# Relative attention: near-diagonal terms for 64 positions at a time over four row groups, and a new table of steps

## The chip, the core and the metric

The kernel runs on one NeuronCore of a Trainium2 chip. Its engines run side by side: TensorE (PE; its weight loads are listed as PEld), VectorE (DVE), ScalarE (ACT), GpSimd (POOL), and SyncE (SP), which starts the DMAs here. Each works through its own instructions in order and waits for others by semaphores. The metric is the device time of one execution in microseconds; 4292.06 us is the median of three runs (4282.06, 4292.06, 4292.41).

## What is computed

Four sublayers on x (16 sequences, 256 positions, 128 features, fp32), each followed by a residual sum and a layer norm: attention with relative positions, a stack of six local-attention layers, a causal attention, and experts. The change touches the first:

```
rel = clip(r[:, None] - r[None, :], -64, 64) + 64
q, k, v = heads(x @ Wq), heads(x @ Wk), heads(x @ Wv)          # 16 heads of 8
content = einsum('bhld,bhmd->bhlm', q, k)
rel_k   = einsum('bhld,lmd->bhlm', q, Ek[rel])
rel_q   = einsum('bhmd,lmd->bhlm', k, Eq[rel])
logits  = (content + rel_k + rel_q + pos_pos) * scale           # pos_pos from Eq, Ek alone
attn    = softmax(logits)
out     = attn @ v + einsum('bhlm,lmd->bhld', attn, Ev[rel])
x       = layernorm(x + out)
```

The terms rel_q and rel_k depend on l - m through a small table that is constant beyond a distance of 64. They are made apart for the two diagonal 128 x 128 blocks of the logits ("near the diagonal") and for corners of the other blocks.

## The kernel before: how the work is staged

`relative_attention` (line 243) works on 16 batches. A batch has eight units: unit u has the 128 rows l of half lc = u // 4 and four heads. Each unit runs three steps: `weights` (L493) builds the logits of four heads in one PSUM tile `big` by transposing the rel_k terms into it (L505) and adding q times k over two 32-row groups of PE (L517), after which DVE adds the rel_q terms and finds the least (L527); `exponentials` (L539) on ACT; `turn_weights` (L552) transposes the result on PE (L562) into two `small` tiles, which ACT or DVE copies out (L566, L568).

PSUM has eight banks: two `big` tiles of two banks each and four `small` tiles of one bank, each kind handed out in turn. A step that takes the next tile of a kind waits until the readers of its last content are done.

Once a batch come the other steps. `turn` and `project` make x transposed, q and k. `diagonal` (L375) multiplies x by spread weights (64 matmuls, L388) and DVE masks the result into the tile `r_d` (L396): in each group of 32 partitions the head features of four neighbouring positions stand block by block, so that one matmul over 32 rows gives the terms of four positions, for all heads and both halves. `diagonal` "k" serves the rel_q terms (`rq_...`), `diagonal` "q" the rel_k terms (`rk_...`); both use the one tile `r_d`. `chunk` (L403) makes the near-diagonal terms of 32 positions: eight matmuls of 32 rows and 128 columns (L413), four quads g times two x, with x in two row groups and two banks of one `big`. `rows_of` (L372) says which row group holds which 16 positions. `rq_chunk` (L445) copies them out by two ACT copies of 128 x 512 (L449), `rk_chunk` (L465) by two DVE additions (L470). Four chunks cover 128 positions, so a batch has four of each. `corners` (L422) makes the other terms, 16 matmuls over all four row groups (L434) a call, two calls of each kind. `positions` (L570), `values` (L606), `join`, `statistics` and `normalise` are the output side; `spread_k` is work of POOL, `project_v` makes v.

The order is written by hand: `TURNS` (L669) has eight turns, one for each unit, and each turn lists its steps with how many units (for the three steps of a unit) or batches they lie behind; -1 means one batch ahead. `run` (L742) goes through the turns, and `in_order` (L204) keeps each of PE, ACT, DVE and POOL in that order. The first four turns run before the last tables are set up (L815), the rest after.

Of the kernel before, what the change touches and what calls it, by code (L numbers as in the profile page):

```python
# [19 lines left out]
P = 128  # L20
NB, S, D = 16, 256, 128
NT = S // P
H, HD = 16, 8
# [81 lines left out]
def bcast(ap, shape):  # L105
    return ap.to_broadcast(list(shape))
# [3 lines left out]
def transformer_kernel(ctx: ExitStack, tc: tile.TileContext, I, out: bass.AP):  # L110
# [93 lines left out]
    def in_order(first):  # L204
# [25 lines left out]
        third=third,  # L230
    )
    relative_attention(tc, I, xb, env)
    wp = ctx.enter_context(tc.tile_pool(name="wp", bufs=2))
    wq = ctx.enter_context(tc.tile_pool(name="wq", bufs=1))
# [8 lines left out]
def relative_attention(tc, I, xb, env):  # L243
# [13 lines left out]
    V, A, G, T = nc.vector, nc.scalar, nc.gpsimd, nc.tensor  # L257
    big, small, ident = env.big, env.small, env.ident
# [3 lines left out]
    C0 = P - 4  # L262
    E0 = MAXD - 4

    with ExitStack() as ctx:
# [5 lines left out]
        rq3, rk3, rkc3 = [None] * 3, [None] * 3, [None] * 3  # L271
# [10 lines left out]
        tq = one.tile([P, NTAB], F32, name="r_tq")  # L282
        tk = one.tile([P, NTAB], F32, name="r_tk")
# [4 lines left out]
        pp = one.tile([P, P], F32, name="r_pp")  # L288
# [19 lines left out]
        def of(three, b, lc):  # L308
            return three[lc * (1 + b % 2)]

        st = {b: {} for b in range(NB)}
# [60 lines left out]
        def rows_of(s_, r):  # L372
            return r if s_ else r ^ 2
# [26 lines left out]
            )  # L400
            st[b]["d", n] = d

        def chunk(table, d, c):  # L403

            ps = big()
            for g in range(4):
                for x in range(2):
                    at = 8 * c + 4 * x + g
                    s_ = at // 16
                    r = rows_of(s_, at // 4 % 4)  # L410
                    o = C0 - 4 * at
                    rows = slice(32 * r, 32 * r + 32)
                    T.matmul(  # L413
                        ps[:, 512 * x + 128 * g : 512 * x + 128 * g + 128],
                        lhsT=table[rows, o : o + P],
                        rhs=d[rows].rearrange("p h t s g i -> p (h t) s g i")[:, :, s_, g, :],
                        start=True,
                        stop=True,
                    )
            return ps  # L420

        def corners(tables, d, halves, upper, phase):  # L422

# [18 lines left out]
                "p x (g h i) -> p x g h i", g=4, i=4  # L442
            )

        def rq_chunk(b, c):  # L445
            ps = chunk(tq, st[b]["d", "k"], c).rearrange("p (g h t i) -> p t g h i", g=8, t=NT, i=4)
            for t in range(NT):
                o = of(rq3, b, t)[:, :, 0, 32 * c : 32 * c + 32]
                A.copy(o.rearrange("p h (g i) -> p g h i", i=4), ps[:, t])  # L449

        def rq_corners(b, phase):

# [9 lines left out]
                    ps[rows],  # L462
                )

        def rk_chunk(b, c):  # L465
            ps = chunk(tk, st[b]["d", "q"], c).rearrange("p (g h t i) -> p t g h i", g=8, t=NT, i=4)
            pc = pp[:, 32 * c : 32 * c + 32].rearrange("p (g i) -> p g i", i=4).unsqueeze(2)
            for t in range(NT):
                o = of(rk3, b, t)[:, :, 32 * c : 32 * c + 32]
                V.tensor_add(  # L470
                    o.rearrange("p h (g i) -> p g h i", i=4), ps[:, t], bcast(pc, (P, 8, H, 4))
                )

        def rk_corners(b, phase):
# [184 lines left out]
        def normalise(b, lc):  # L659
# [8 lines left out]
        UNIT = (weights, exponentials, turn_weights)  # L668
        TURNS = (  # L669
            (  # L670
                (1, values, 0),
                (0, rk_corners, 1),
                (-1, turn),
                (0, rk_chunk, 1),
                (2, turn_weights),
                (0, rk_chunk, 0),
                (0, rk_corners, 0),
                (-1, project),
                (1, exponentials),
                (-1, diagonal, "k"),  # L680
                (0, weights),
            ),
            (
                (2, turn_weights),
                (0, weights),
                (1, exponentials),
            ),
            (
                (0, weights),
                (1, positions, 1),  # L690
                (2, turn_weights),
                (1, join, 0),
                (1, exponentials),
            ),
            (
                (1, exponentials),
                (0, weights),
                (-1, rq_chunk, 1),
                (1, values, 1),
                (2, turn_weights),  # L700
                (-1, rq_corners, 1),
                (-1, rq_chunk, 2),
            ),
            (
                (1, exponentials),
                (1, join, 1),
                (0, weights),
                (-1, rq_chunk, 0),
                (2, turn_weights),
                (-1, spread_k, 0),  # L710
            ),
            (
                (2, turn_weights),
                (1, exponentials),
                (1, statistics, 1),
                (0, weights),
            ),
            (
                (-1, rq_chunk, 3),
                (0, positions, 0),  # L720
                (1, normalise, 1),
                (-1, rq_corners, 0),
                (1, exponentials),
                (-1, diagonal, "q"),
                (0, weights),
                (-1, rk_chunk, 3),
                (2, turn_weights),
                (0, project_v),
                (1, statistics, 0),
            ),  # L730
            (
                (1, exponentials),
                (2, turn_weights),
                (0, weights),
                (1, normalise, 0),
                (-1, spread_k, 1),
                (-1, rk_chunk, 2),
            ),
        )
        N = NB * NU  # L740
# [13 lines left out]
        with tc.tile_pool(name="r_setup", bufs=1) as su, tc.tile_pool(  # L754
# [32 lines left out]
            def toeplitz(dst, ext):  # L787

                ps = small()
                for j in range(4):  # L790
                    o = S - 1 - C0 - j
                    T.matmul(
                        ps[:, 0:NTAB],
                        lhsT=sel[:, j, :],
                        rhs=ext[:, o : o + NTAB],
                        start=(j == 0),
                        stop=(j == 3),
                    )
                V.tensor_scalar_mul(dst, ps[:, 0:NTAB], -scale)
                return ps  # L800

            ps = toeplitz(tq, extq)
# [22 lines left out]
            ps = small()  # L825
# [38 lines left out]
            for dst, n, src, d, width, parts, end in (  # L864
# [6 lines left out]
                for i in range(0, width, 512):  # L871
                    n_ = min(512, width - i)
                    ps = small()
# [1083 lines left out]
```

## Time and profile before

| | |
|---|---|
| median of three runs | 4292.06 us |
| profiled execution, its own time | 4290.48 us |
| span of its profile, first to last instruction | 4288.7 us |
| relative attention on PE | from 17 to 820 us |
| PE, DVE, ACT, POOL busy in 85 to 820 us | 719.65, 442.50, 448.80, 143.53 us of 735 |
| matmul records of `chunk` (L413) in 85 to 775 us | some 1,870, 0.27 us each by the record |
| granted PE clock 25 to 38, 38 to 47, 47 to 62 us | 0.61, 0.64, 0.53 |
| granted PE clock 85 to 820 us | 1.00 |

An fp32 matmul leaves two records. Records overlap, since PE is pipelined: what a step costs PE is the time from its first start to the next step's first start, and this is what the prediction uses. A line of the timeline merges neighbouring records of one line of code: start, length, engine, line, operation, output and inputs, contraction rows * columns of the weights, shape of the moving operand, count. "issue" is idle time in which the engine waited for nothing that the profile shows.

### The profile page before, as it was taken

How to read it: one execution, taken by the hardware profiler on the slowest of the kernel's cores; microseconds unless marked ns; L12 is line 12 of the kernel's file. 1: busy time of each engine (PE TensorE's matmuls, PEld its weight loads, DVE VectorE, ACT ScalarE, POOL GpSimd, SP SyncE). 2: the span in 40 equal slices, each digit the busy share in tenths (PEclk: the TensorE clock that was granted, in tenths of full speed). 3: DMA queues.
4: the chain of work that ended last, by engine and by line, in shares of the span. 5: the costliest groups of instructions: out<-in, count | busy, mean ns of one | idle time of the engine just before them, and what ended most of it. 6: DMA issues, size and time to landing. Idle time of an engine off the chain costs nothing.

```text
span 4288.7 us, 149072 instructions
## 1 busy us (share of the span) xinstructions
PE 4167.7 (97%) x62028; PEld 3051.9 (71%) x62028; DVE 3321.3 (77%) x6347; ACT 3293.4 (77%) x11368; POOL 2698.4 (63%) x3176
## 2 busy tenths in 40 slices
PE   8999999889999999999999999999999999989997
PEld 6888888667677777667776677776766777656665
DVE  4655665588888888888888888888888888769974
ACT  3666566488888888888888888888888888769973
POOL 2121211388888888888888888888888888623321
PEclk8999999999999999999999999999999999989998
DMA  1000000100000000000000000000000000000000
GB/s 35 3 3 3 3 3 3 49 25 15 20 20 23 19 20 19 25 19 15 20 19 24 20 21 19 24 18 16 19 15 24 15 15 14 9 2 2 2 8 20
DMA packets 158799, 69.51 MB, mean 16 GB/s; under 512 B 123549, under 2 KB 154276, under 8 KB 158124
## 3 DMA queue, kind: packets, MB, share of 16 engines
q1 hardware_dynamic: 158124, 59.99, 5.6%
q8 instruction: 488, 8.00, 0.8%
q14 instruction: 187, 1.53, 0.1%
HBM read 21.72 MB, written 2.12 MB: 6 GB/s over the span
## 4 chain that ended last, share of the span: by engine, by line
PE 91%; POOL 3%; issue 2%; ACT 2%; DVE 2%; DMA 0%; SPq 0%; POOLq 0%; ACTq 0%; DVEq 0%
PE small L1240 15%; PE big L1090 15%; PE small L1147 7%; PE big L1215 7%; PE big L1162 6%; PE small L1215 3%; PE small L1337 3%; PE small L1321 3%; PE big L505 3%; PE small L562 3%; PE small L1578 3%; PE small L1305 3%; PE big L1534 3%; PE big L517 3%; PE big L413 2%
## 5 line engine op out<-in xcount | busy, mean ns | idle before, releaser
L1183 ACT ACTIVATE a_pr<-a_pr,a_nb 128x64 f32<-128x64 f32 x3072 | 1023.8, 338 | 6.6 <-DVE a_nb L1176 6.6
L1111 POOL TENSOR_TENSOR a_u<-a_u,a_r 128x1024 f32<-128x1024 f32 x384 | 900.7, 2367 | 51.9 <-DVE a_r L1106 51.9
L1129 POOL TENSOR_TENSOR a_u<-a_u,a_y 128x1024 f32<-128x1024 f32 x384 | 722.4, 1902 | 15.0
L1240 PE MATMUL small<-a_vo,a_g 128*128 128x128 f32 x6144 | 719.2, 275 | 2.6 <-ACT a_g L1233 2.6
L1240 PEld LDWEIGHTS small<-a_vo,a_g 128*128 128x128 f32 x6144 | 702.6, 192 | 4.5 <-ACT a_g L1233 4.4
L1101 ACT ACTIVATE a_sq<-big 128x1024 f32<-128x1024 f32 x384 | 391.1, 1020 | 304.8 <-PE big L1090 304.5
L1183 ACT ACTIVATION_READ_ACCUMULATOR a_pr<-a_pr,a_nb 128x1 f32 x3072 | 587.9, 191 | 0.0
L1118 DVE TENSOR_REDUCE a_ss<-a_sq 128x16 f32<-128x1024 f32 x384 | 446.6, 1202 | 0.0
L1147 PE MATMUL small<-ident,a_u 128*128 128x128 f32 x3072 | 402.3, 274 | 12.9 <-POOL a_u L1129 12.9
L1090 PE MATMUL big<-w_k,a_xs 128*128 128x512 f32 x768 | 385.4, 624 | 2.2 <-DMA w_k<-in_L_ffn_Wqkv_dram 1.7
L1147 PEld LDWEIGHTS small<-ident,a_u 128*128 128x128 f32 x3072 | 346.4, 141 | 50.6 <-POOL a_u L1129 32.4
L1195 POOL TENSOR_TENSOR a_pr<-a_pr,a_rd 128x1024 f32<-128x1024 f32 x192 | 365.5, 1904 | 16.7 <-DVE a_rd L1194 16.5
L1090 PE MATMUL big<-w_q,a_xs 128*128 128x512 f32 x768 | 360.9, 592 | 0.0
L1162 PEld LDWEIGHTS big<-a_kT,a_qT 64*32 64x32 f32 x24576 | 262.5, 105 | 130.0 <-issue 71.1
L1170 DVE TENSOR_TENSOR a_pr<-big,w_band 128x1024 f32<-128x1024 f32 x192 | 234.7, 1222 | 110.4 <-PE big L1162 110.4
L527 DVE CUSTOM_DVE_ANT_0 r_lg<-big,r_rq 128x256 f32<-128x256 f32 x512 | 186.9, 421 | 155.5 <-PE big L517 67.4
L1162 PE MATMUL big<-a_kT,a_qT 64*32 64x64 f32 x24576 | 295.5, 226 | 10.5 <-POOL a_kT L1140 5.5
L1102 DVE TENSOR_TENSOR a_u<-big,a_tak 128x1024 f32<-128x1024 f32 x192 | 235.0, 1224 | 86.3 <-ACT a_sq L1101 82.8
L1223 ACT COPY a_g<-big 128x1024 f32<-128x1024 f32 x192 | 194.4, 1012 | 115.8 <-PE small L1215 115.2
L1215 PE MATMUL small<-a_pT,a_xm 32*128 32x512 f32 x768 | 282.4, 643 | 0.2 <-DVE xa L1247 0.2
L1090 PEld LDWEIGHTS big<-w_q,a_xs 128*128 128x128 f32 x768 | 145.5, 190 | 185.2 <-issue 129.5
L1215 PE MATMUL small<-a_pT,a_xt 32*128 32x512 f32 x768 | 262.8, 592 | 0.0
(276 smaller groups left out, 9482.0 us busy)
## 6 DMA issues: line engine op xcount, KB each, us to landing
a_xm<-a_xt SPq DMA_DIRECT2D x96, 96.0 KB
f_xt<-xa SPq DMA_DIRECT2D x96, 64.0 KB
f_xt<-xa SPq DMA_DIRECT2D x96, 63.5 KB
a_xt<-xa SPq DMA_DIRECT2D x80, 64.0 KB
a_xt<-xa SPq DMA_DIRECT2D x80, 63.5 KB
w_k<-in_L_ffn_Wqkv_dram SPq DMA_DIRECT2D x6, 512.0 KB
w_q<-in_L_ffn_Wqkv_dram SPq DMA_DIRECT2D x6, 512.0 KB
w_v<-in_L_ffn_Wqkv_dram SPq DMA_DIRECT2D x6, 512.0 KB
```

What stands on the lines that cost most here:

```text
L1090: T.matmul(ps[:, c * 512 : (c + 1) * 512], lhsT=xs_of[i, b][:, t, 0:P], rhs=weights[i]["qk"[j]][:, c * 512 : (c + 1) * 512], start=True, s ...
L1101: A.activation(sq, ps3, AF.Square)
L1102: V.tensor_mul(u, ps3, bcast(ta[:, t].unsqueeze(1), (P, H, DH)))
L1111: G.tensor_add(u, u, r)
L1118: V.tensor_reduce(ss[:, j], st[m]["sq", j], AX.X, ALU.add)
L1129: G.tensor_mul(u, u, bcast(y[:, j].unsqueeze(2), (P, H, DH)))
L1147: T.transpose(ps[:, k, :], u[:, o : o + P], ident)
L1162: T.matmul(ps[q0 : q0 + WIN, e, c, :], lhsT=qT[DH * e : DH * (e + 1), c, q0 : q0 + WIN], rhs=kT[DH * e : DH * (e + 1), c, t * P + q0 : t * ...
L1183: A.activation(s_["pr"][:, h], s_["pr"][:, h], AF.Exp, bias=s_["nb"][:, h : h + 1], accum_out=s_["den"][:, h : h + 1],)
L1195: G.tensor_mul(s_["pr"], s_["pr"], bcast(rd.unsqueeze(2), (P, H, DH)))
L1215: T.matmul(ps[win], lhsT=x[r, t, :], rhs=pT[r, :, o, :], start=(o == 0), stop=(o == 1),)
L1240: T.matmul(ps[:, 0:D], lhsT=st[m]["g"][:, h, :], rhs=weights[i]["vo"][:, h // 2, h % 2, :], start=(h == 0), stop=(h == H - 1),)
```

## The change

`chunk` becomes `diagonals`, which makes the terms of 64 positions in one go: 16 matmuls of the same shape, in the order quad g, then c over the four row groups. Group c writes its own bank: two of one `big`, and two `small` tiles. The evictions go tile by tile: for the `big` two instructions of 128 x 512 elements, for each `small` two of 128 x 256, six a half in place of four for two chunks. `rq_chunk` and `rk_chunk` become `rq_half` and `rk_half`, two of each for a batch. `TURNS` is written anew: the halves stand in turns 4 and 5 (rq), 7 and 0 (rk), and other steps move too: `values` and `diagonal` "k" in turn 0, `join`, `rq_corners`, `rk_corners`, `spread_k`, `diagonal` "q", `positions`, `statistics`, `normalise` and `project_v` as the diff shows. The sum of the matmuls and of the elements evicted stays.

```diff
--- before.py
+++ after.py
@@ -400,24 +400,29 @@
             )
             st[b]["d", n] = d
 
-        def chunk(table, d, c):
-
-            ps = big()
+        def diagonals(table, d, s_):
+
+
+
+            both = big()
+            ps = [both[:, 0:512], both[:, 512:1024], small(), small()]
             for g in range(4):
-                for x in range(2):
-                    at = 8 * c + 4 * x + g
-                    s_ = at // 16
-                    r = rows_of(s_, at // 4 % 4)
-                    o = C0 - 4 * at
+                for c in range(4):
+                    r = rows_of(s_, c)
+                    o = C0 - 4 * (16 * s_ + 4 * c + g)
                     rows = slice(32 * r, 32 * r + 32)
                     T.matmul(
-                        ps[:, 512 * x + 128 * g : 512 * x + 128 * g + 128],
+                        ps[c][:, 128 * g : 128 * g + 128],
                         lhsT=table[rows, o : o + P],
                         rhs=d[rows].rearrange("p h t s g i -> p (h t) s g i")[:, :, s_, g, :],
                         start=True,
                         stop=True,
                     )
-            return ps
+            for n, p_ in ((8, both), (4, ps[2]), (4, ps[3])):
+                at = 64 * s_ + (0 if n == 8 else 32 if p_ is ps[2] else 48)
+                p_ = p_.rearrange("p (g h t i) -> p t g h i", g=n, t=NT, i=4)
+                for t in range(NT):
+                    yield t, at, n, p_[:, t]
 
         def corners(tables, d, halves, upper, phase):
 
@@ -442,11 +447,10 @@
                 "p x (g h i) -> p x g h i", g=4, i=4
             )
 
-        def rq_chunk(b, c):
-            ps = chunk(tq, st[b]["d", "k"], c).rearrange("p (g h t i) -> p t g h i", g=8, t=NT, i=4)
-            for t in range(NT):
-                o = of(rq3, b, t)[:, :, 0, 32 * c : 32 * c + 32]
-                A.copy(o.rearrange("p h (g i) -> p g h i", i=4), ps[:, t])
+        def rq_half(b, s_):
+            for t, m0, n, p_ in diagonals(tq, st[b]["d", "k"], s_):
+                o = of(rq3, b, t)[:, :, 0, m0 : m0 + 4 * n]
+                A.copy(o.rearrange("p h (g i) -> p g h i", i=4), p_)
 
         def rq_corners(b, phase):
 
@@ -462,13 +466,12 @@
                     ps[rows],
                 )
 
-        def rk_chunk(b, c):
-            ps = chunk(tk, st[b]["d", "q"], c).rearrange("p (g h t i) -> p t g h i", g=8, t=NT, i=4)
-            pc = pp[:, 32 * c : 32 * c + 32].rearrange("p (g i) -> p g i", i=4).unsqueeze(2)
-            for t in range(NT):
-                o = of(rk3, b, t)[:, :, 32 * c : 32 * c + 32]
+        def rk_half(b, s_):
+            for t, l0, n, p_ in diagonals(tk, st[b]["d", "q"], s_):
+                pc = pp[:, l0 : l0 + 4 * n].rearrange("p (g i) -> p g i", i=4).unsqueeze(2)
+                o = of(rk3, b, t)[:, :, l0 : l0 + 4 * n]
                 V.tensor_add(
-                    o.rearrange("p h (g i) -> p g h i", i=4), ps[:, t], bcast(pc, (P, 8, H, 4))
+                    o.rearrange("p h (g i) -> p g h i", i=4), p_, bcast(pc, (P, n, H, 4))
                 )
 
         def rk_corners(b, phase):
@@ -668,73 +671,69 @@
         UNIT = (weights, exponentials, turn_weights)
         TURNS = (
             (
-                (1, values, 0),
                 (0, rk_corners, 1),
                 (-1, turn),
-                (0, rk_chunk, 1),
                 (2, turn_weights),
-                (0, rk_chunk, 0),
-                (0, rk_corners, 0),
+                (0, rk_half, 0),
                 (-1, project),
+                (-1, diagonal, "k"),
+                (1, values, 0),
                 (1, exponentials),
-                (-1, diagonal, "k"),
                 (0, weights),
             ),
             (
+                (0, weights),
                 (2, turn_weights),
-                (0, weights),
-                (1, exponentials),
-            ),
-            (
-                (0, weights),
-                (1, positions, 1),
-                (2, turn_weights),
-                (1, join, 0),
                 (1, exponentials),
             ),
             (
                 (1, exponentials),
                 (0, weights),
-                (-1, rq_chunk, 1),
-                (1, values, 1),
+                (1, positions, 1),
                 (2, turn_weights),
-                (-1, rq_corners, 1),
-                (-1, rq_chunk, 2),
             ),
             (
                 (1, exponentials),
-                (1, join, 1),
+                (1, join, 0),
                 (0, weights),
-                (-1, rq_chunk, 0),
+                (-1, rq_corners, 1),
+                (1, values, 1),
                 (2, turn_weights),
-                (-1, spread_k, 0),
             ),
             (
-                (2, turn_weights),
+                (1, join, 1),
+                (-1, rq_corners, 0),
                 (1, exponentials),
                 (1, statistics, 1),
                 (0, weights),
+                (-1, rq_half, 0),
+                (2, turn_weights),
             ),
             (
-                (-1, rq_chunk, 3),
-                (0, positions, 0),
+                (0, weights),
+                (2, turn_weights),
                 (1, normalise, 1),
-                (-1, rq_corners, 0),
+                (0, project_v),
                 (1, exponentials),
-                (-1, diagonal, "q"),
-                (0, weights),
-                (-1, rk_chunk, 3),
-                (2, turn_weights),
-                (0, project_v),
                 (1, statistics, 0),
+                (-1, rq_half, 1),
             ),
             (
+                (-1, diagonal, "q"),
+                (2, turn_weights),
                 (1, exponentials),
+                (0, weights),
+            ),
+            (
+                (0, weights),
+                (-1, rk_corners, 0),
+                (-1, spread_k, 1),
                 (2, turn_weights),
-                (0, weights),
+                (-1, spread_k, 0),
+                (-1, rk_half, 1),
+                (0, positions, 0),
+                (1, exponentials),
                 (1, normalise, 0),
-                (-1, spread_k, 1),
-                (-1, rk_chunk, 2),
             ),
         )
         N = NB * NU
```

## The prediction

> **What bounds the kernel now.** I read the page first, then busy time by stretch, then the timeline of one period of the relative attention, where the change lies.
>
> ```profile
> span 4288.7 us, 149072 instructions
> PE 4167.7 (97%) x62028; PEld 3051.9 (71%) x62028; DVE 3321.3 (77%) x6347; ACT 3293.4 (77%) x11368; POOL 2698.4 (63%) x3176
> ...
> q8 instruction: 488, 8.00, 0.8%
> ```
>
> PE is the busiest engine of the page. The stretch 85 to 770 us, which is the steady part of the relative attention, says it more sharply (columns: stretch, length, busy us and count of PE, PEld, DVE, ACT, POOL, then clock and DMA):
>
> ```profile
> 85.00:770.00 685.00, 672.00 (x15020) 585.49 (x15024) 414.50 (x1423) 421.94 (x1323) 137.63 (x225) 1.00 0.01 3
> ```
>
> PE is busy 672 of 685 us, DVE and ACT 60%. The timeline of PE (start, length, line, shape, count; two records to one matmul) shows steps set end to end; one batch takes 47.6 us from `diagonal` k at 440.50 to the next at 488.09, the mean over batches is 48.1. So a change is worth what it does to the PE sequence, as long as PE doesn't begin to wait.
>
> ```profile
> 399.35 0.60 PE L517 MATMUL big<-r_ks,r_qe 32*128 32x256 f32 x4
> 399.88 0.66 PE L505 MATMUL big<-ident,r_rk 128*128 128x128 f32 x4
> ...
> 405.48 0.60 PE L505 MATMUL big<-ident,r_rkc 128*128 128x128 f32 x4
> 406.01 0.48 PE L517 MATMUL big<-r_ks,r_q 32*128 32x256 f32 x2
> 406.04 0.49 PE L413 MATMUL big<-r_d,r_tq 32*128 32x128 f32 x4
> 406.33 0.38 PE L517 MATMUL big<-r_ks,r_q 32*128 32x256 f32 x2
> 406.36 0.39 PE L413 MATMUL big<-r_d,r_tq 32*128 32x128 f32 x4
> ...
> 407.13 1.96 PE L614 MATMUL small<-r_pT,r_spread 128*32 128x128 f32 x64
> ...
> 410.98 0.69 PE L434 MATMUL big<-r_d,r_tqc 32*64 32x64 f32 x32
> 411.60 1.16 PE L413 MATMUL big<-r_d,r_tq 32*128 32x128 f32 x16
> 412.69 0.33 PE L642 MATMUL small<-ident,r_oT 128*128 128x128 f32 x1
> ...
> 421.66 1.09 PE L388 MATMUL big<-r_xT,r_wrepq 128*32 128x64 f32 x60
> 423.21 1.20 PE L388 MATMUL big<-r_xT,r_wrepq 128*32 128x64 f32 x68 [0.46 <-issue]
> ```
>
> Two things are to be seen. At 406 the chunk (L413) written behind `weights` runs *among* its L517 matmuls: they sit in two of the four row groups, the chunk in the other two, and both end at 407.13. And at 423.21 `diagonal` q stops in its middle, with nothing waited for.
>
> **Part 1, the matmuls.** A chunk alone takes 1.09 us (411.60 to 412.69) for 16 records in two row groups: eight rounds of 0.112 us and 0.2 us to begin. The same chunk behind `weights` costs nothing: 405.046 to 407.129 is 2.08 us for both, and `weights` alone takes 2.08 (397.85 to 399.88, 2.03, where another follows). By order of the steps four of eight chunks are so placed (rq 1, 0, 3; rk 2). rk 3 at 426.33 shares the groups of its `weights` and adds 0.90. So eight chunks cost 4 x 0 + 0.90 + 3 x 1.09 = **4.17 us** a batch.
>
> The new half has 32 records, a quarter for each row group: eight rounds again, if four groups stream at once. At 406 four did, with 128 columns, into four banks; L434 at 410.98 runs 32 records in four groups in 0.62 us. So 1.09 us each. Three stand alone (behind `turn_weights` or `project_v`, which use all rows). rq_half 0 follows `weights` of unit 4 in groups 0 and 1: its records there come after, as with rk 3, so 0.90. Sum: 0.90 + 3 x 1.09 = **4.17 us**. The packing gains nothing: what it packs together was already hidden, four times of eight. Bounds: 3.2 (rq_half 0 hidden) to 4.6.
>
> **Part 2, neighbours.** The new table changes which kinds follow each other. From start-to-start times: `turn` before a chunk 0.37, before a full-row step about 0.22; a join behind a chunk 0.27, behind transposes 0.11; `values` before `corners` 2.97, before full-row work 2.88; `diagonal` k before `weights` 1.925, and before `values` (same column shape) some 0.08 less. All rows of the new order sum to 46.50 us a batch against 46.85 of the old one without stops: **-0.35 us**; bounds 0 and -0.5.
>
> **Part 3, evictions and waits.** ACT: each rq half has two copies of 512 and four of 256 elements. By rows 0.53 us start to start (L449) and 0.27 to 0.30 (L329): 2.2 us against 2.1 for two chunks. DVE: two adds of 0.62 (L470) and four of about 0.35 (between L643's 0.28 for 128 and L470's 0.68 for 512; the bounds are these two): 2.6 against 2.5. Both have 40% to spare, so this costs only where PE waits for a bank. A half takes both banks of one `big` and two of the four `small`. I laid the steps out with these rows, 0.15 us from PE to a reader and 0.1 back. ACT is the close one: after `weights` of unit 3 ends (0), `rq_corners` 1 is copied 1.6 to 2.7, oT, two turned tiles to 5.2, `rq_corners` 0 to 6.6, exp of unit 3 to 8.6, rq_half 0 to 10.9, turned tiles to 13.0, exp of unit 4 to 15.0, rq_half 1 to 17.4. PE wants rq_half 1's first `small` at 12.85 (free at 12.5), exp of unit 4 at 15.85, `weights` of unit 6 its `big` at 16.8 (free at 16.1). Margins 0.3 to 0.8 us: no wait. One place is short: rk_half 1 needs the `big` that DVE (L527, four of 0.345) reads for unit 7, free 1.75 us after `weights`, wanted at 1.65. **+0.1 us**; bounds 0 and +1.0 (each 256-wide copy as long as a 512-wide one). `spread_k` 0 moves from turn 4 to turn 7: POOL has 5.4 us of both there, and their reader in turn 0 is 13 us off; without that cover it would cost 2.7 us. The DMAs don't move. Where `diagonal` k comes next, DVE's mask multiply of 1.22 us ends 1.2 us before `weights`.
>
> **Part 4, the stop at 423.21.** Every long gap inside L388 lies at the same place of a 256-instruction block of PE's stream (weight loads and matmuls counted), and q8's 488 packets make 8.00 MB, 16 KB or 256 instructions each.
>
> ```profile
> engine line waited for: us in total, times, longest us
> PE big L388 <- issue: 12.1, 16, 1.9
> ```
>
> The packet records show the block's fetch starting at 420.73, landing at 421.77, and PE going on at 423.21; all stops end 2.4 to 2.7 us after their fetch starts. The fetches start about 1.2 us after PE comes within some 20 matmuls of the block before. So I take: if the last 148 matmuls ran in less than 3.7 us, PE stops for the rest. `diagonal` q runs a matmul in 15 ns, `corners` before it in 19.5, `positions` before that in 21: at its 60th record that is 0.90 + 0.62 + 1.19 = 2.71 us, a stop of 1.0 (measured 0.68; at the 98th 1.2 counted, 2.1 measured). Over all positions this gives 1.07 us a batch; measured, `diagonal` q and k exceed 1.925 us by 17.6 us in 15 batches, 1.15 each. In the new order `diagonal` q follows rq_half 1 (34 ns a record) and `project_v`: only its last 20 records are short, 0.11 us on the mean. But `diagonal` k is now followed by `values` (29 ns), whose first 70 records fall short by 0.7 us: 0.39. With small ones 0.60. **-0.55 us** a batch; bounds +0.2 and -1.15.
>
> The Trainium skill ("Runtime: NRT & Kernel Launch", Instruction fetch mechanics) says that blocks of 256 instructions are fetched while the one before executes and that this is hidden by the sequencer's issue rate. The block size agrees with this trace, the hiding doesn't: L388 lost 12.1 us. By that rule this part is zero and the sum -6.3 instead of -14.5.
>
> **Part 5, the beginning.** Between the first `diagonal` q's multiply and the first `weights` (47.70 to 62.16 us) four rk chunks stand at a granted clock of 0.53 (stretch 47 to 62) with waits, 3.55 us a pair; two halves of about 1.8 us and one wait give 12 us for 14.5: **-2.5 us**; bounds +2 and -5 (PE also reaches the setup's matmuls at 30.03 some 1.6 us earlier).
>
> **The sum.** Fifteen batches: 15 x (-0.35 + 0.1 - 0.55) = -12.0, and -2.5 at the start: -14.5 us. The profiled execution took 4290.48 us (span 4288.7 and 1.8 around it): **4276 us**. The median of the runs shown is 4292.06 (4282.06 to 4292.41), so -0.37%. A measurement of this kernel tells about 0.3% from no change: below 4279 or above 4305.
>
> **Rivals.** (a) The fetch stops only move, to `values` behind `diagonal` k: -6.3 us, 4284. For it: two dense steps stand together there; against it: `values` runs at half the rate of `diagonal`. (b) They vanish: -24, 4267. (c) ACT comes late at the three places of Part 3 by the upper bound, 1 us a batch: 4290. (d) Slower: four row groups don't stream four different 128-column loads at once, and a half goes as two chunks, 2.0 us. From the second round on PE would pay: 4 x 0.9 x 15.5 = +56 us, 4332. Against it stand 406.01 and L434; but no row has one step in four groups at 128 columns. (e) Chunks behind `weights` aren't really free, and the four that were unpacked save 4 x 1.09 us: -65, 4211.
>
> The skill ("TensorE: Matmul & The Clock Gate", Part 3) says that matmuls start and end in program order; by it (e) would hold. The L517 and L413 records at 406 interleave, against it.
>
> **Chances.** Forecast 0.45, own range 4268 to 4285, two thirds of it below 4279; (a) 0.18; (b) 0.18; (c) 0.11; (d) 0.06; (e) 0.02. Faster 0.30 + 0.18 + 0.02 = 0.50; within 0.3%: 0.15 + 0.18 + 0.11 = 0.44; slower 0.06. Range 4262 to 4297: from (b) less its scatter to (c) plus the spread of the runs.
>
> **What would show it.** In the new profile: L413's successor with 32 records in 1.09 us; a period of 47.2 us (rival (d): 50.8); `diagonal` q at 1.93 us in most batches, and gaps by "issue" at `values` of unit 0's turn; PE waiting for ACT or DVE nowhere but about 0.1 us before rk_half 1. PE waits of over 0.3 us by `small` or `big` would prove Part 3 wrong.

## The result and the profile after

The kernel after takes **4267.31 us** (median of six runs, 4263.78 to 4275.0), the kernel before on the same chip 4290.02 us (median of six, 4282.06 to 4292.41). The ratio is 0.9952, 95% interval 0.9939 to 0.9965: 0.5% faster, where 4276 us and -0.37% were forecast. The profiled execution of the kernel after is the slowest of its six: 4275.0 us, span 4273.2.

The page of the kernel after, its first part and the queue of PE's instruction fetches:

```profile
span 4273.2 us, 149121 instructions
PE 4155.3 (97%) x62028; PEld 3024.7 (71%) x62028; DVE 3327.6 (78%) x6411; ACT 3307.4 (77%) x11432; POOL 2703.2 (63%) x3176
...
q8 instruction: 488, 8.00, 0.8%
```

PE has the same 62028 records and the same 488 blocks of instructions, and 64 more instructions each on DVE and ACT. In the stretch 85 to 770 us it is even fuller than before (columns as in the prediction):

```profile
85.00:770.00 685.00, 677.42 (x15229) 576.37 (x15221) 428.81 (x1510) 433.58 (x1403) 141.70 (x230) 1.00 0.01 3
```

677 of 685 us are busy, and 15229 records are done where there were 15020. From one `diagonal` k to the next a batch takes 47.2 to 47.4 us in three profiles of this kernel (47.37, 47.21, 47.33 on the mean; forecast 47.2), 48.1 before.

Two more views of the kernel after answer to those of before. First the timeline of PE around `rq_half` 1 and `diagonal` q:

```profile
405.06 0.61 PE L353 MATMUL small<-r_wv,r_xT 128*128 128x128 f32 x4
405.60 0.38 PE L414 MATMUL big<-r_d,r_tq 32*128 32x128 f32 x2
405.61 0.38 PE L414 MATMUL small<-r_d,r_tq 32*128 32x128 f32 x2
...
406.48 0.28 PE L414 MATMUL big<-r_d,r_tq 32*128 32x128 f32 x2
406.50 0.28 PE L414 MATMUL small<-r_d,r_tq 32*128 32x128 f32 x2
406.70 1.99 PE L388 MATMUL big<-r_xT,r_wrepq 128*32 128x64 f32 x128
408.63 0.55 PE L565 MATMUL small<-ident,r_lg 128*128 128x128 f32 x3
```

The half (L414) runs in rounds 0.11 us apart, in each round two records into `big` and two into the `small` tiles: four row groups at once. From 405.60 to 406.70 it takes 1.10 us (1.09 forecast). `diagonal` q behind it runs through in 1.93 us, with no stop. Then PE's waits from 80 to 770 us:

```profile
engine line waited for: us in total, times, longest us
PE small L617 <- issue: 1.8, 4, 0.6
PE big L388 <- issue: 1.5, 2, 0.8
PE small L628 <- ACT r_oT L625: 0.7, 1, 0.7
```

The 12.1 us by "issue" at L388 are 1.5, and the first line is now L617, `values`. The list holds the longer waits only; step by step, the stops that "issue" names come to 0.63 to 0.74 us a batch, where there were 1.3.

### The profile page after: what moved, and what is told of

It reads as the page before. It is cut to its first block, busy times and chain, and to the rows that moved or that the text cites. A ratio compares the mean times of both kernels' runs of the same rounds, so it can differ in the third digit from the quotient of the medians.

```text
span 4273.2 us, 149121 instructions
## 1 busy us (share of the span) xinstructions
PE 4155.3 (97%) x62028; PEld 3024.7 (71%) x62028; DVE 3327.6 (78%) x6411; ACT 3307.4 (77%) x11432; POOL 2703.2 (63%) x3176
## 4 chain that ended last, share of the span: by engine, by line
PE 91%; POOL 3%; issue 2%; DVE 2%; ACT 2%; DMA 0%; SPq 0%; POOLq 0%; ACTq 0%; DVEq 0%
PE small L1239 15%; PE big L1089 15%; PE small L1146 7%; PE big L1214 6%; PE big L1161 6%; PE small L1214 3%; PE big L520 3%; PE small L1336 3%; PE small L1320 3%; PE small L565 3%; PE small L1577 3%; PE big L508 3%; PE small L1304 3%; PE big L1533 3%; PE big L388 1%
## 5 line engine op out<-in xcount | busy, mean ns | idle before, releaser
L1182 ACT ACTIVATION_READ_ACCUMULATOR a_pr<-a_pr,a_nb 128x1 f32 x3072 | 601.0, 196 | 0.0
L1146 PE MATMUL small<-ident,a_u 128*128 128x128 f32 x3072 | 402.6, 274 | 14.5 <-POOL a_u L1128 14.5
```

Of the source, the lines that this page charges most:

```text
L1146: T.transpose(ps[:, k, :], u[:, o : o + P], ident)
L1182: A.activation(s_["pr"][:, h], s_["pr"][:, h], AF.Exp, bias=s_["nb"][:, h : h + 1], accum_out=s_["den"][:, h : h + 1],)
```

## The experiments

Ratios are to the kernel before on the same chip; "period" is a batch in the steady part, and "without stops" is the sum over its steps of each step's undisturbed time: 46.82 us for the kernel before, 46.58 for the one after. The theory is that of the prediction: packing by itself gains nothing, the new order gains by better neighbours and by moving the dense matmuls away from places where PE runs out of fetched instructions.

**1. The changed kernel again.** No edit.

> The changed kernel as it is, once more: a second profile and more times. Theory 1 (the gain is 0.85 us a batch in the steady part, from 0.25 us by neighbours and 0.6 us by shorter instruction-fetch stops, and the rest from a start that met fewer slow clock windows): steady period 47.2 to 47.4 us again with the stops at about 0.7 us a batch; the first weights step at 54.5 us again if the start's clock follows from the order of the steps, anywhere between 54 and 60 us if it is chance. Theory 2 (packing over four row groups makes the gain): the same period; it tells nothing apart. Time 4264 to 4275 us for both.

Measured: 4266.48 us against 4281.92, ratio 0.9963 (0.9951 to 0.9975). The gain repeats on a second chip, smaller (15.4 us between the medians, 22.7 on the first); period 47.21 us.

**2. The new table with the old chunks.**

```diff
         def rq_half(b, s_):
-            for t, m0, n, p_ in diagonals(tq, st[b]["d", "k"], s_):
-                ...
+            rq_chunk(b, 2 * s_)
+            rq_chunk(b, 2 * s_ + 1)
```

(and `rk_half` likewise, with the chunks of the kernel before)

> The new table of steps, but each half made by two chunks of 32 positions over two row groups, one behind the other. Theory 1: a half stands where only rq 0 can run beside a weights step; chunks cost 7 x 1.09 us a batch in place of 4.17, so +3.46 us a batch, less some 0.3 us of stops in the thinner stream: +48 us, 4315 us (4305 to 4325), slower than before too: the new table needs the packing, though the packing by itself gains nothing against the old table. Theory 2 (the table alone makes the gain, and chunks hide or cost little wherever they stand): 4267 us.

Measured: 4395.88 us, ratio 1.0269 (1.0255 to 1.0282). The waits of PE from 90 to 800 us, and busy PE and granted clock of this kernel around one pair of chunks:

```profile
PE big L388 <- ACT r_rq L449: 18.1, 12, 1.5
PE big L413 <- DVE r_nb L535: 16.9, 12, 1.4
```

```profile
461.40:468.30 6.90, 5.49 (x93) 1.00 0.01 2
468.30:471.70 3.40, 3.40 (x18) 0.50 0.00 0
```

The direction was right, the size was far off: 129 us above the changed kernel on the first experiment's chip. Two chunks in a row need both `big` tiles, and the second waits for one: 1.4 us before L413, 1.5 us before `diagonal` q. The four places take 5.02, 3.27, 2.39 and 1.73 us where halves take 2.98, 1.10, 1.10 and 1.10: +6.1 us a batch, some 92 us in all. And within 2 us of ten of these 24 waits the granted clock falls to half, mostly for one piece of 3.4 us (second fence): 81.9 us of half clock up to the last `join`, against 10.2 in the changed kernel; with half the speed lost, that is at most 36 us more. Together these come to 128 us, enough for the 129, though the 36 is a bound and wasn't measured.

**3. The old table with `diagonal` q moved.** It stands behind `turn_weights`, where PE has run slower matmuls before it; `rk_chunk` 3 follows later.

```diff
                 (1, exponentials),
-                (-1, diagonal, "q"),
                 (0, weights),
-                (-1, rk_chunk, 3),
                 (2, turn_weights),
+                (-1, diagonal, "q"),
                 (0, project_v),
...
                 (2, turn_weights),
+                (-1, rk_chunk, 3),
                 (0, weights),
```

> The old kernel and table, but diagonal q stands behind weights and turn_weights of its turn and no longer right behind positions and corners; rk chunk 3 goes behind turn_weights of the next turn. Theory 1: the stops in diagonal q (1.1 us a batch) go, because the 148 matmuls up to its end now take over 3.7 us; rk chunk 3 costs 1.09 us in place of 0.90, and its wait for the mask some 0.15 us: -0.8 us a batch, -12 us, 4278 us (4272 to 4285). Rival (the fetch of instructions is short of its mean rate and a stop that is taken away comes back at another dense step): the stops stay at 1.1 to 1.3 us a batch, 4290 to 4295 us.

Measured: 4286.84 us, ratio 1.0013 (1.0005 to 1.0022). PE's timeline:

```profile
421.29 1.09 PE L562 MATMUL small<-ident,r_lg 128*128 128x128 f32 x8
422.32 1.99 PE L388 MATMUL big<-r_xT,r_wrepq 128*32 128x64 f32 x128
...
428.40 0.37 PE L517 MATMUL big<-r_ks,r_qe 32*128 32x256 f32 x1
...
428.69 0.86 PE L413 MATMUL big<-r_d,r_tk 32*128 32x128 f32 x12
429.49 1.96 PE L614 MATMUL small<-r_pT,r_spread 128*32 128x128 f32 x64
```

`diagonal` q takes 1.92 us in every batch (3.03 before), and all stops together fall from 1.3 to 0.33 us a batch: the mechanism of Part 4 acts as it was read. A small part moved: in two of 13 batches PE now stops 1.4 and 1.6 us in or just behind `diagonal` k, where the kernel before lost 0.1 us a batch. The time still doesn't fall, since the period without stops rises by 1.06 us to 47.88. Half of that is in the last lines: `rk_chunk` 2 waits for a bank behind `weights`, so that twelve of its records stick out, and the pair takes 2.64 us for 2.08; the rest is `rk_chunk` 3 alone (+0.10) and the neighbours.

**4. The old table with `rk_chunk` 1 and 3 exchanged**, so that the one behind `weights` of unit 6 lies in the free row groups.

```diff
-                (0, rk_chunk, 1),
+                (0, rk_chunk, 3),
...
-                (-1, rk_chunk, 3),
+                (-1, rk_chunk, 1),
```

> The old kernel and table with rk chunks 1 and 3 exchanged, nothing else: chunk 1 uses row groups 0 and 1 and now stands behind the weights step of unit 6, which uses groups 2 and 3. Theory 1 (a chunk in the two groups that weights leaves free costs nothing): -0.90 us a batch, -13.5 us, 4276 us (4270 to 4282). Rival (PE runs matmuls in program order, and the interleaved records mislead): no change, 4290 us.

Measured: 4278.44 us, ratio 0.999 (0.9982 to 0.9999). PE, then DVE:

```profile
419.18 0.70 PE L517 MATMUL big<-r_ks,r_q 32*128 32x256 f32 x4
419.55 0.38 PE L413 MATMUL big<-r_d,r_tk 32*128 32x128 f32 x2
419.72 0.38 PE L517 MATMUL big<-r_ks,r_qe 32*128 32x256 f32 x2
419.77 0.39 PE L413 MATMUL big<-r_d,r_tk 32*128 32x128 f32 x4
419.94 0.38 PE L517 MATMUL big<-r_ks,r_qe 32*128 32x256 f32 x2
419.99 0.72 PE L413 MATMUL big<-r_d,r_tk 32*128 32x128 f32 x10
420.64 1.09 PE L562 MATMUL small<-ident,r_lg 128*128 128x128 f32 x8
```

```profile
418.27 1.22 DVE L396 TENSOR_TENSOR r_d<-big,r_mask 128x1024 f32<-128x1024 f32 x1 [2.57 <-PE big L388]
```

The chunk runs among the L517 records, so program order doesn't forbid it; but its operand `r_d` is ready at 419.49, and it begins at 419.55, in the middle of the L517 records that began at 419.18. Ten of its sixteen records start after the last of these. `weights` and chunk take 2.48 us where 2.98 were: half of the cover, -0.49 us a batch without stops. The medians differ by 3.5 us only, where 15 x 0.49 are 7.4; the traced execution, 4270.77 us, is the third fastest of twelve, and no trace shows the slower ones.

**5. The packing alone: the old table with halves** at the places of rq chunks 0 and 3, rk half 1 for chunk 3, rk half 0 for chunk 1; the other four chunks taken out of the table.

```diff
-                (-1, rq_chunk, 0),
+                (-1, rq_half, 0),
...
-                (-1, rq_chunk, 3),
+                (-1, rq_half, 1),
...
-                (-1, rk_chunk, 3),
+                (-1, rk_half, 1),
...
-                (0, rk_chunk, 1),
+                (0, rk_half, 0),
```

> The packing alone: halves over four row groups in the old table, at the places of rq chunks 0 and 3, rk chunk 3 and rk chunk 1; the other chunks go. Theory 1: three halves behind a weights step cost 0.90 us each and one 1.09, 3.79 us a batch in place of 4.17; diagonal q keeps its stops of 1.1 us a batch: -0.4 us a batch, -6 us against the kernel before (0 to -12; the start may add -5). Theory 2 (packing over four row groups makes the gain): -0.85 us a batch and more, -16 to -22 us, as the changed kernel.

Measured: 4305.45 us against 4285.27, ratio 1.0053 (1.0037 to 1.0069), on the other side of what was expected. PE's waits from 90 to 740 us:

```profile
PE small L565 <- ACT r_rq L453: 8.3, 13, 0.6
PE small L565 <- DVE r_rk L473: 7.5, 12, 0.7
PE big L388 <- issue: 6.9, 11, 1.6
PE small L353 <- ACT r_pT L569: 2.9, 12, 0.2
```

A half holds two of the four `small` tiles, and here `turn_weights` (L565) comes for them before the copies are done: 0.6 and 0.7 us a batch, and `project_v` (L353) 0.2. The period is about 50 us, 1.8 more than with chunks.

**6. The changed kernel with rq half 0 as two chunks**, each behind a `weights`, and four steps shifted to make room.

```diff
                 (0, weights),
+                (-1, rq_chunk, 1),
+                (1, values, 1),
                 (-1, rq_corners, 1),
-                (1, values, 1),
...
-                (1, join, 1),
                 (-1, rq_corners, 0),
+                (1, join, 1),
...
                 (0, weights),
-                (-1, rq_half, 0),
+                (-1, rq_chunk, 0),
                 (2, turn_weights),
...
-                (0, weights),
                 (2, turn_weights),
+                (0, weights),
```

> The changed kernel with rq half 0 given back as two chunks of two row groups, chunk 1 behind the weights step of unit 3 and chunk 0 behind that of unit 4, each in the groups that weights leaves free; rq corners and one turn_weights change places with neighbours so that no bank is waited for. Theory 1 (beside weights a chunk is free, so hiding beats packing): rq costs 1.10 us a batch and at most 0.3 of waits in place of 2.0: -0.6 to -0.8 us a batch, -9 to -12 us against the changed kernel, -26 us against the kernel before. Theory 2 (packing gains): slower than the changed kernel by 0 to 10 us.

Measured: 4275.4 us, ratio 0.9974 (0.9966 to 0.9983). Chunk 1 is free (2.08 us with its `weights`), chunk 0 adds 0.70; other rows get longer by changed neighbours (`turn_weights` behind `corners` +0.15, `project_v` +0.10, `rq_half` 1 +0.09, the end of `values` +0.09). The rows sum to 46.74 us without stops, 0.16 above the changed kernel, and stops rise to 1.2 us a batch: 0.36 at `values`, 0.20 in `diagonal` q, 0.35 in `turn_weights` behind it. Hiding a chunk doesn't pay here, since the changed neighbours and the new stops cost more.

**7. Row groups in turn**: the loops of `diagonals` exchanged, so that four matmuls of one row group follow each other.

```diff
-            for g in range(4):
-                for c in range(4):
+            for c in range(4):
+                for g in range(4):
```

> The changed kernel, but in a half the four matmuls of one row group stand together, group after group, in place of one of each group in turn. If PE lets row groups run ahead of each other within its queue, as chunk and weights did (64 weight loads and matmuls a half): 1.1 to 1.4 us a half, 0 to +1.2 us a batch, 4266 to 4285 us. If matmuls start in program order: each group's eight records run alone, 0.9 us and four of them, 3.6 us a half: +2.5 us each, +10 us a batch, +150 us, 4420 us.

Measured: 4373.2 us, ratio 1.0205 (1.019 to 1.0221). One half of this kernel:

```profile
464.67 1.37 PE L414 MATMUL big<-r_d,r_tq 32*128 32x128 f32 x13
465.78 0.37 PE L414 MATMUL small<-r_d,r_tq 32*128 32x128 f32 x1
465.88 0.27 PE L414 MATMUL big<-r_d,r_tq 32*128 32x128 f32 x1
...
466.22 1.27 PE L414 MATMUL small<-r_d,r_tq 32*128 32x128 f32 x13
```

Records run one after another 0.11 us apart; only at the seam of two groups do some overlap. A half takes 2.75 us, between the two expectations. Three of them at 2.75 for 1.10 and `weights` with a half at 4.10 for 2.98 make +6.1 us a batch, and nine of 14 periods are 52.58 us (46.58 + 6.1 = 52.65, without any stop). So the four groups stream together in the changed kernel *because* consecutive matmuls go to different groups.

**8. `values` apart from `diagonal` k**, against the new stops at `values`.

```diff
                 (2, turn_weights),
+                (1, values, 0),
                 (0, rk_half, 0),
                 (-1, project),
                 (-1, diagonal, "k"),
-                (1, values, 0),
```

> The changed kernel with values 0 moved in front of rk half 0, so that it no longer stands right behind diagonal k. Theory 1 (a stop where 148 matmuls take under 3.7 us): the stops at values (0.35 us a batch) go, diagonal k pays 0.11 for the change of shape behind it: the sum of stops 0.3 us a batch in place of 0.65, -0.25 us a batch, -3 to -6 us against the changed kernel. Rival (fetches are short on the mean and stops only move): stops of 0.6 us a batch elsewhere, +1 to +3 us.

Measured: 4267.96 us, ratio 0.9962 (0.9948 to 0.9976), no different from the changed kernel. The stops at `values` are gone (all stops from 0.63 to 0.4 us a batch), and the rows lose 0.28: `diagonal` k before `weights` 1.925 for 1.811, the end of `values` 1.09 for 0.995, `weights` 2.085 for 2.03.

**9. Experiments 6 and 8 together.**

> The sixth experiment's order with values of half 0 ahead of the rk half, as in the eighth. Theory (each edit acts by itself): the sixth's period without stops, about 46.1 us, gains the 0.28 us that the eighth's change of neighbours cost, 46.4; of its 1.2 us of stops the 0.36 at values and part of those behind them go, 0.75 left: a period of 47.15 us, one or two us below the changed kernel, a ratio to the kernel before of 0.996. Rival (stops move on to the next dense stretch): stops stay at 1.2 us, period 47.6, ratio 0.998.

Measured: 4276.51 us against 4286.42, ratio 0.9972 (0.996 to 0.9983). The 46.1 us in the expectation was misread: the sixth's rows sum to 46.74. With that base the theory's steps hold (rows 47.04, +0.30 for 0.28; stops 0.6 to 0.7, for 0.75), and the period is 47.7 us. The ratio lies between the theory's 0.996 and the rival's 0.998, and its interval holds both; it is the stops, 0.6 to 0.7 us and not 1.2, that speak against the rival. No order tried here beats the changed kernel.

**10 and 11. Both kernels again, for the beginning.** No edits.

> The kernel before, unchanged, for its beginning. Theory (the time to the first weights follows from how long the granted clock stays at half, which is partly chance): slow clock ahead of the first join other than 30.7 us, and the first weights earlier or later with it, anywhere in 55 to 63 us. Rival (the order of the steps sets it): 30 us at half clock and the first weights at 62 us again.

> The changed kernel, unchanged, for its beginning, and to see how much of the span lies behind the last join of the relative attention. Theory (chance): slow clock other than 10.2 us, first weights anywhere in 53 to 58 us; the remainder anywhere in 3459 to 3473 us. Rival (order): 10 us at half clock and the first weights at 53.5 to 54.5 us a third time.

Measured: 4290.79 and 4269.75 us, one run each; spans 4289.0 and 4268.0. Busy PE and granted clock by stretches, the first and second profile of before, then the first and third of after:

```profile
46.00:50.00 4.00, 2.57 (x40) 0.50 0.00 0
50.00:54.00 4.00, 3.55 (x54) 0.50 0.02 4
```

```profile
46.00:50.00 4.00, 2.57 (x48) 0.50 0.00 0
50.00:54.00 4.00, 3.55 (x54) 0.50 0.02 4
```

```profile
46.00:50.00 4.00, 3.21 (x108) 1.00 0.00 0
50.00:54.00 4.00, 3.89 (x163) 1.00 0.01 4
```

```profile
46.00:50.00 4.00, 3.25 (x95) 1.00 0.02 4
50.00:54.00 4.00, 3.57 (x137) 1.00 0.01 4
```

My theory of chance fell for this stretch. The kernel before shows half clock in both profiles, the changed one full clock in all three. From the first `diagonal` q to the first `weights` before takes 19.53 and 19.52 us, after 11.89, 11.87 and 11.88. In these five profiles the beginning goes with the program. That it always does isn't shown: both profiles of before have a mean granted clock of 0.984, and other executions of the same kernel, which have no trace, reach 0.988 (4274.51 us).

Elsewhere the same program does differ. At 520 us PE stops for 1.56 us at the same place in both profiles of before; then the first goes on at full clock, the second at half. PE's timeline, then busy PE and granted clock, of the first:

```profile
520.59 0.43 PE L388 MATMUL big<-r_xT,r_wrepq 128*32 128x64 f32 x16 [1.56 <-issue]
522.20:529.00 6.80, 6.80 (x104) 1.00 0.00 1
```

and of the second:

```profile
520.46 0.43 PE L388 MATMUL big<-r_xT,r_wrepq 128*32 128x64 f32 x16 [1.56 <-issue]
522.20:529.00 6.80, 6.80 (x42) 0.50 0.00 1
```

## Why the prediction was right, and which term was not

**What bounds it.** Right: PE is busy 677 of 685 us, and what changed on PE changed the time.

**Part 1, the matmuls.** Right to 0.05 us: a half alone 1.103 us (1.09), `weights` with `rq_half` 0 2.98 us (2.08 + 0.90). Rival (d), halves that run as two chunks, would have given a period of 50.8; the seventh experiment shows that its mechanism exists, at another order of the loops. That the packing by itself gains nothing the fifth shows: in the old table it costs 0.5%. But the second shows that the new table can't do without it: with chunks it costs 2.7%. As tried here, neither part of the change is a gain; the pair is.

**Parts 2 and 3.** Right in sum: rows of 46.58 us for 46.82, -0.24 a batch, where -0.35 + 0.10 was forecast. The one wait named is the one that is there: `turn_weights` before `rk_half` 1 takes 1.215 us for 1.022, so 0.19 rather than 0.1 us. No other wait for ACT or DVE recurs. The list puts 0.7 us at L628 down to ACT; three profiles of this kernel have such a gap there (0.66, 0.37 and 0.64 us, at 188 to 190 us), but it stands at the same place of PE's 256-instruction blocks as the gaps by "issue", so it is one more stop of Part 4. By the records the DVE add of 256 elements takes 0.42 us, 0.33 start to start where 0.35 was estimated. Rival (c) would have shown as 1 us a batch at three places; none of them waits.

**Part 4, the stops.** Right, with two small misreadings (17.6 us in 15 batches are 1.17 each, not 1.15, and the stops end 2.3 to 2.9 us after their fetch starts, not 2.4 to 2.7): `diagonal` q 3.03 us on the mean before, 2.04 to 2.08 after; the new ones stand at `values`, 0.33 to 0.37 us a batch (0.39 forecast), in PE's timeline of the kernel after:

```profile
422.69 1.99 PE L388 MATMUL big<-r_xT,r_wrepk 128*32 128x64 f32 x128
424.50 0.82 PE L617 MATMUL small<-r_pT,r_spread 128*32 128x128 f32 x19
425.64 1.51 PE L617 MATMUL small<-r_pT,r_spread 128*32 128x128 f32 x45 [0.33 <-issue]
```

The sum is 0.63 to 0.74 for the 0.60 forecast. What caused it is shown from three sides: moved among slower matmuls, `diagonal` q stops nowhere (third experiment), `values` taken from behind `diagonal` k doesn't stop there (eighth), and where the halves ahead of both `diagonal` steps take two and a half times as long, nine periods have none at all (seventh). Rival (a), stops that only move, is out, but for the small part that turned up at `diagonal` k in the third. Rival (b) had them vanish and gave 4267 us, which is the time measured; but they didn't vanish, and that it agrees is a coincidence of two other sums.

**Part 5, the beginning: the mis-sized term.** The step was "four rk chunks stand at a granted clock of 0.53 ... two halves of about 1.8 us and one wait give 12 us for 14.5: -2.5 us". It took the clock of before as given. The stretch that it names, 14.46 us before, takes 8.46 us after (46.03 to 54.49): -6.0 us. With `diagonal` q ahead of it, it is -7.65 us, past my bound of -5. The fourth experiment splits it, by one trace: there the same count of chunks stands between the same steps, the clock is at half for only 1.7 us from the first `diagonal` q on (18.5 before), and from there to the first `weights` it takes 14.24 us, 5.3 less than before. A pair of chunks takes 2.63 us there, where it took 3.55. From 14.24 to 11.88 are -2.4 us, and 0.7 of these lie in `diagonal` q, which began at half clock in the fourth; the halves in place of pairs give the other -1.6 (10.07 to 8.46 us). That is less than the -2.5 forecast for them, which was worked out at half clock. The remaining 6.0 of the 7.65 us go with the clock. What decides it isn't settled: in one profile each, exchanging two chunks (fourth) or moving `diagonal` q (third: 17.17 us, half clock for two pieces from 50.4) went with a faster one, and I found no rule that gives the pieces from the steps.

**The sum.** The median, 4267.31 us, lies inside the whole range but 0.7 us below the forecast's own, 4268 to 4285. 15 x -0.85 and -7.65 are -20.4 us. In the traces the last `join` starts 19.3 us earlier in the pair first compared (800.5 for 819.8). The agreement is rough: cut at `diagonal` k, the first two periods give -8.1 and -5.2, the next thirteen -9.9, and what stands before and behind them +0.8 and +3.1. In the tenth and eleventh experiment the last `join` starts 26.9 us earlier (799.0 for 825.9), but two batches of the kernel before took 52.55 and 52.42 us there, 3.5 and 3.6 more than in its first profile, each with half clock for 6.83 us: 7.1 of the 26.9 aren't the change.

The code behind the last `join`, the same in all, took 3472.7 us after and 3468.9 before in the first pair, 3468.9 after and 3463.1 before in the second; over all thirteen profiles it lies between 3459.4 and 3472.7. I take that for scatter between executions. So the spans differ by 15.5 us in the first pair and by 21.0 in the second, and that the second is near the sum is luck. The medians differ by 22.7 us on the first chip and by 15.4 on the second (first experiment); no trace shows which part of the time is smaller there.

## What to carry to other kernels

Price a repacking with its table: what it packs may already have been hidden, and the tiles it takes from other steps cost more than the matmuls it saves, unless the order is made for it. Where PE is full, cost each step by the time from its start to the next one's start, by its neighbours too: this sum was right to 0.1 us in 47, and changes of order that each looked free cost 0.05 to 0.15 us each. A stretch at half clock isn't a fixed background: ask what the change does to the clock there, and compare several profiles of each kernel before calling it chance, or the program.

## What the runs showed of the hardware

- **Instruction fetch is not always covered.** PE stops at one place of its 256-instruction blocks, mostly where the 148 matmuls before it took under 3.7 us, 25 ns each. In the kernel before, from 85 to 760 us, 15 of 18 such places have a stop of over 0.12 us, and 2 of the other 98; in the kernel after 9 of 13, and 2 of 105. They come to 1.3 us a batch before, 0.63 to 0.74 after, 0.33 in the third experiment, with 488 blocks in each page. A profile can put such a stop down to another engine (L628 above).
- **Four row groups stream together when consecutive matmuls alternate between them, and hardly when four of one group stand in a row**: 32 records in 1.10 us with the groups interleaved, in 2.75 with four matmuls of a group in a row. The Trainium skill ("TensorE: Matmul & The Clock Gate", Part 3) says that weight loads overlap with running matmuls of other row groups, while matmuls start and end in program order. The seventh experiment is near that: overlap only at the seams. The fourth is not: the chunk is written after all of the L517 matmuls, and six of its records start before the last two of theirs.
- **The granted clock moves in pieces of 3.41 us**, and in the second experiment ten of 24 waits of 1.1 to 1.6 us in the steady part were followed by such a piece at half clock, or by two or three. The length of the wait alone doesn't decide: after the same stop of 1.56 us one profile of the kernel before has half clock, the other doesn't. The Trainium skill ("TensorE: Matmul & The Clock Gate", Part 1) gives a window of 3.4 us, which agrees; it also calls the beginning variable from run to run, and that these profiles don't show: 19.53 and 19.52 us, and 11.87 to 11.89, over the same steps.
